# Layer 1 of a four-layer graph network as a nested polynomial in adj, two pairs of batches at a time, and the comparisons and mask values of the softmax on GpSimd

## The chip, the cores and the metric

The kernel runs on one core of one Trainium2 chip. The metric is the device time of a whole execution in microseconds (us). Runs are compared with runs of the kernel before, taken on the same chip in the same rounds.

## The reference, cut to what matters

`x` has 32 batches of 512 nodes and 128 features; `adj` is a sparse, non-negative 512x512 matrix. Each of four layers is a layer norm, a ReLU, a graph operation and a residual.

```python
# layer 0: a softmax over the columns where adj > 0; entry number k in row order gets e[k]
m = adj > 0
idx = jnp.cumsum(m.reshape(-1).astype(jnp.int32)) - 1
vals = e[0][idx].reshape(adj.shape)          # e has 256 entries, later ones repeat the last
A = jax.nn.softmax(jnp.where(m, vals, NEG), axis=1)
out = einsum('ij,bjg->big', A * M, h0) + einsum('ij,bjg->big', A * (1.0 - M), h1) + bias
# layer 1: Chebyshev hops of order 2, for A1 = A2 = adj
x1 = einsum('bnf,nw->bwf', x0, A)
x2 = 2.0 * einsum('bnf,nw->bwf', x1, A) - x0
out = relu(concat(X, x1, x2, x1, x2) @ Theta1 + bias)
# layer 2: messages through adj * adj (elementwise), two projections;  layer 3: masked attention
```

## The kernel before: the parts that matter

Two batches form a pair `q`, 16 pairs in all. A product with a 512x512 matrix is a seven-product scheme over 2x2 blocks. Three banks (a, c, d) take the seven products, and a bank is written again as soon as its reader has taken the last sum out:

```python
ORDER = ((1, "a", True), (6, "c", True), (5, "d", True), (7, "c", False), (2, "a", False),
         (4, "c", False), (3, "d", False))

def products(name, form, left, right, evict):
    banks = {}
    for k, g, first in ORDER:
        if first:
            banks[g] = bank(f"p_{name}_{g}")
        form(banks[g], left[k], right[k], first)      # TensorE
        evict(k, banks[g])                            # VectorE, or ScalarE for 1 and 2
        yield
```

Layer 1 forms `cheb` = 2 adj^2 - 1 once and then, for each pair, multiplies by adj and by cheb, **interleaved two by two**:

```python
def layer1(q):
    h = normed(q)
    yield
    hT = transposed(h, f"hT1_{q}")                    # VectorE and DMA
    right = right_blocks(..., f"h_{q}", [nc.gpsimd] * 4)  # four differences on GpSimd, rt_h
    yield
    mixes = (mixed(f"x1T_{q}", sums["adj"], right, x1T, ...),
             mixed(f"x2T_{q}", sums["cheb"], right, x2T, ...))
    for _ in zip(*mixes):
        pass
    hs = [straight(hT, b, None, f"hs_{q}_{b}") for b in range(2)]
    yield
    for b in range(2):                                # three projections, summed in a bank
        po = projected(..., (columns(hs[b]), th[:, 0, :]), (columns(x1T[:, b]), th12[:, 0, :]),
                       (columns(x2T[:, b]), th12[:, 1, :]))
        ...                                           # bias, relu, residual on VectorE
    ln_stats(q)
```

The softmax preparation, cut to the four comparisons and the values of unmasked entries:

```python
for t in range(NT):
    s = prep.tile([P, NE], F16, tag="lt", name=f"lt_{t}", bufs=2)
    nc.vector.tensor_scalar(s, cols[:, :NE], incl[:, t : t + 1], None, OP.is_lt)
    nc.vector.scalar_tensor_tensor(of_row[:, t, :], cols[:, :NE], before[:, t : t + 1], s,
                                   OP.is_ge, OP.mult)
...
nc.tensor.matmul(ph, identh, m[:, t, :], start=False, stop=True)   # the mask, for each t
```

The order of work between the layers is that of a list of generators; each step of the list advances all active ones in turn, and an engine takes its instructions in the order in which they were issued (some reordering by a scheduler apart):

```python
waiting = [[next_layer, layer0_last(), layer1(1)]]
waiting += [[layer1(q)] for q in range(2, NQ)]
waiting[5].append(square())
waiting[-1].insert(0, layer2(0))                      # layer 2 begins ahead of layer 1's last pair
waiting += [[layer2(q)] for q in range(1, NQ)]
```

## Time and profile before

| Landmark in the trace (us from the span's start) | before |
|---|---|
| row counts of adj known (`incl`) | 7.43 |
| first product of layer 0 | 35.74 |
| second product of layer 0 | 40.05 |
| first product of layer 1 | 196.49 |
| first score product of layer 3 | 686.91 |
| end of the span | 972.16 |
| **median time of three runs** | **974.61** |

The landmarks are the starts of records in TensorE's timeline (`incl` is from VectorE's). They cut the span into parts, so that a change of the total can be put down to a part. The profile's other lines stand in the prediction. Columns are start, us, engine, line, operation, tiles, shapes, records and, in brackets, the idle time before and its releaser.

### The profile page before, as it was taken

To read this page: it belongs to the slowest core of one execution; us is meant where nothing else is said; L and a number is where in the kernel's file an instruction comes from. 1 tells how busy PE (TensorE), PEld (TensorE's weight loads), DVE (VectorE), ACT (ScalarE), POOL (GpSimd) and SP (SyncE) were. 2 spreads that over 40 slices of the span, in tenths; PEclk is the share of its full clock that TensorE was granted. 3 is DMA by queue.
4 is the path that set the end of the run, shared out by engine and by line. 5 is a ranking of instruction groups with operands and counts; after the bars stand their busy time and mean duration, and the time that the engine had idled before them with its cause. 6 is when DMAs were issued, how large, how long until landed. Compare 5 with 4: busy or idle time off the path is not lost.

```text
span 972.2 us, 15193 instructions
## 1 busy us (share of the span) xinstructions
PE 963.8 (99%) x5477; PEld 786.5 (81%) x5478; DVE 591.7 (61%) x1367; ACT 467.6 (48%) x1056; POOL 396.4 (41%) x447
## 2 busy tenths in 40 slices
PE   8999999999999999999999999999999999999998
PEld 4789999899999999999977777777676777777776
DVE  8768887755555655557756666656554444444444
ACT  5765456022323223248676644455674455444553
POOL 5658798932244222221244443334142333223322
DMA  9155554511241221235343433332132121121111
GB/s 261 49 152 152 153 151 116 145 37 51 97 121 44 71 61 50 81 87 140 80 123 114 126 94 87 86 87 75 54 91 64 45 76 55 55 77 44 55 33 44
DMA packets 83050, 87.10 MB, mean 90 GB/s; under 512 B 6816, under 2 KB 73120, under 8 KB 82976
## 3 DMA queue, kind: packets, MB, share of 16 engines
q1 hardware_dynamic: 82976, 86.14, 31.3%
q8 instruction: 43, 0.70, 0.3%
q14 instruction: 31, 0.25, 0.1%
HBM read 44.70 MB, written 41.42 MB: 89 GB/s over the span
## 4 chain that ended last, share of the span: by engine, by line
PE 95%; DVE 2%; ACT 1%; POOL 0%; DMA 0%; issue 0%; DVEq 0%; ACTq 0%
PE p_av L956 12%; PE p_l L406 12%; PE p_score L941 11%; PE p_msgT_c L351 5%; PE p_x1T_c L351 4%; PE p_x2T_c L351 4%; PE p_l_c L358 4%; PE p_feat L406 3%; PE p_msgT_d L351 3%; PE p_x1T_a L351 3%; PE p_msgT_a L351 3%; PE p_hv L406 3%; PE p_x2T_d L351 3%; PE p_x1T_d L351 3%; PE p_x2T_a L351 3%; PE p_g L406 3%
## 5 line engine op out<-in xcount | busy, mean ns | idle before, releaser
L233 ACT ACTIVATE h<-x,sh,rs 128x128 f32<-128x128 f32 x512 | 208.8, 483 | 90.0 <-PE p_x2T_d L351 46.6
L946 POOL TENSOR_TENSOR ex<-ex,adjTx 128x512 f32<-128x512 f32 x64 | 83.2, 1301 | 206.4 <-ACT ex L944 200.8
L942 ACT ACTIVATE ex<-p_score 128x512 f32<-128x512 f32 x128 | 71.9, 587 | 124.6 <-issue 113.0
L956 PEld LDWEIGHTS p_av<-qkh_hv,ex 128*128 128x128 f32 x1024 | 118.5, 191 | 9.4 <-issue 7.4
L956 PE MATMUL p_av<-qkh_hv,ex 128*128 128x129 f32 x1024 | 120.1, 275 | 0.8 <-POOL ex L946 0.8
L941 PE MATMUL p_score<-qkh_hv,hT 128*128 128x512 f32 x256 | 115.2, 593 | 0.0
L267 DVE STREAM_TRANSPOSE hb_hT<-h 128x512 f32<-128x512 f32 x122 | 83.1, 696 | 20.0 <-ACT h L233 18.5
L946 DVE TENSOR_TENSOR ex<-ex,adjTx 128x512 f32<-128x512 f32 x64 | 45.4, 709 | 81.8 <-ACT ex L944 81.8
L205 DVE BATCH_NORM_STATS2 bn<-x 128x6 f32<-128x256 f32 x256 | 93.0, 418 | 1.6
L941 PEld LDWEIGHTS p_score<-qkh_hv,hT 128*128 128x128 f32 x256 | 46.2, 190 | 46.5 <-issue 45.0
L406 PE MATMUL p_l<-th,x12T 128*128 128x128 f32 x512 | 78.1, 275 | 0.0
L944 ACT ACTIVATE ex<-ex 128x512 f32<-128x512 f32 x128 | 76.6, 630 | 1.9
L332 POOL TENSOR_TENSOR rt_h<-h 128x256 f32<-128x256 f32 x32 | 23.3, 727 | 114.2 <-PE p_x2T_d L351 66.8
L406 PEld LDWEIGHTS p_l<-th,x12T 128*128 128x128 f32 x512 | 67.5, 192 | 0.0
L332 POOL TENSOR_TENSOR rt_feat<-feat,feat 128x256 f32<-128x256 f32 x16 | 11.6, 727 | 126.1 <-ACT feat L894 126.1
L666 POOL COPY hs<-hT 128x512 f32<-128x512 f32 x32 | 19.6, 614 | 74.5 <-PE p_l L406 32.9
L406 PE MATMUL p_l<-th,hs 128*128 128x128 f32 x256 | 49.5, 275 | 0.0
L406 PEld LDWEIGHTS p_hv<-vw,hT 128*128 128x128 f32 x256 | 33.6, 192 | 15.3 <-issue 8.1
L906 POOL TENSOR_TENSOR x<-x,phi2b 128x256 f32<-128x256 f32 x64 | 45.0, 735 | 0.0
L379 ACT COPY x12T<-p_x1T_a 128x256 f32<-128x256 f32 x16 | 6.0, 372 | 74.5 <-PE p_x1T_a L351 74.5
L406 PEld LDWEIGHTS p_l<-th,hs 128*128 128x128 f32 x256 | 40.0, 192 | 0.8
L961 DVE SCALAR_TENSOR_TENSOR x<-p_av,rsum,x 128x128 f32<-128x128 f32 x128 | 39.1, 347 | 1.9
(225 smaller groups left out, 1978.6 us busy)
## 6 DMA issues: line engine op xcount, KB each, us to landing
d_hT<-hb_hT SPq DMA_DIRECT2D x244, 128.0 KB
hT<-d_hT SPq DMA_DIRECT2D x61, 512.0 KB
x<-in_x_dram SPq DMA_DIRECT2D x32, 256.0 KB
out_dram<-x SPq DMA_DIRECT2D x31, 256.0 KB
adj_s<-in_adj_dram SPq DMA_DIRECT2D x4, 256.0 KB
adjT_d<-adjT SPq DMA_DIRECT2D x1, 1024.0 KB
sq<-in_adj_dram SPq DMA_DIRECT2D x4, 256.0 KB
adjTx<-adjT_d SPq DMA_DIRECT2D x4, 256.0 KB
```

What stands on the lines that cost most here:

```text
L205: nc.vector.bn_stats(st[:, k].rearrange("p e s -> p (e s)"), xt[q][:, b, t : t + 2, :].rearrange("p t f -> p f t"))
L233: nc.scalar.activation(h[:, b, t, :], xt[q][:, b, t, :], AF.Relu, bias=shift[q][:, i : i + 1], scale=scale[q][:, i : i + 1])
L267: nc.vector.transpose(hb[:, :, b].rearrange("p j t r -> p t j r"), h[:, b].rearrange("p t (j c) -> p t j c", c=QR))
L351: nc.tensor.matmul(p[:, :H], b[:, k, :], a[:, k, :], start=(first and k == 0), stop=(k == 1), skip_group_check=True)
L406: nc.tensor.matmul(p[:, blk(t)], hT(t), w, start=(i == 0), stop=(i == len(terms) - 1))
L906: tc.keep_in_program_order(nc.gpsimd.tensor_add(xi, xi, spread(phi2b, 2)))
L941: nc.tensor.matmul(ps, hT[:, t, b, :], qkh, start=True, stop=True)
L942: nc.scalar.activation(ex[:, t, :], ps, AF.Tanh, scale=1.0 / (8.0 * math.sqrt(D)))
L944: nc.scalar.activation(ex[:, t, :], ex[:, t, :], AF.Exp, scale=8.0)
L946: eng.tensor_mul(ex[:, t, :], ex[:, t, :], adjTx[0][:, t, :])
L956: nc.tensor.matmul(po[:, i, : D + 1], ex[:, t, blk(i0 + i)], hv[:, t, :], start=(t == 0), stop=(t == NT - 1))
L961: nc.vector.scalar_tensor_tensor(xi, po[:, i, :D], rsum[:, i0 + i : i0 + i + 1], xi, OP.mult, OP.add)
```

## The change

Layer 1 is written as x Theta' + adj (x Theta'' + adj x Theta'''), so that adj squared is never formed. For two pairs at a time, one multiplication by adj gives x1T, a two-term projection gives `w`, ScalarE copies it out, GpSimd forms its four differences, and a second multiplication by adj gives tokens, to which the own term is added. Every multiplication by adj now stands alone. In the softmax, the comparisons go to GpSimd, and so does adding the unmasked entries' value to the mask (`entries`), which saves a TensorE product for each row block. The transposes of adj move behind the counts. Cut to its core:

```diff
-    s = prep.tile([P, NE], F16, tag="lt", name=f"lt_{t}", bufs=2)
-    nc.vector.tensor_scalar(s, cols[:, :NE], incl[:, t : t + 1], None, OP.is_lt)
+    s = prep.tile([P, NE], F16, tag="lt", name=f"lt_{t}", bufs=4)
+    nc.gpsimd.tensor_scalar(s, cols[:, :NE], incl[:, t : t + 1], None, OP.is_lt)
 ...
+    def entries(t):
+        nc.scalar.mul(us[t], m[:, t, :], elastn)
+        nc.gpsimd.tensor_add(att[:, t, :], us[t], att[:, t, :])
 ...
-        nc.tensor.matmul(ph, identh, m[:, t, :], start=False, stop=True)
 ...                                        # cheb_rows and its calls go
-    def layer1(q):
-        ...
+    def layer1(r):                          # pairs A = 2r and C = 2r + 1
+        h[A] = normed(A)
+        yield
+        turned(A)                           # transpose by DMA, rt_h on GpSimd
+        h[C] = normed(C)
+        yield
+        first(A)                            # mixed(x1T), alone
+        turned(C)
+        yield
+        first(C)
+        weighed(A)                          # two-term projection, nc.scalar.copy to w1
+        yield
+        weighed(C)
+        right2 = right_blocks(... w1 ..., f"w_{r}", [nc.gpsimd] * 4)     # rt_w
+        yield
+        for _ in products(f"l1_{r}", by_token, sums["adj"], right2, evict):
+            pass
+        ...                                 # own term, bias, relu, residual, statistics
-    waiting = [[next_layer, layer0_last(), layer1(1)]]
-    waiting += [[layer1(q)] for q in range(2, NQ)]
+    waiting = [[next_layer, layer0_last()], [layer1(1)]]
+    for r in range(2, NQ // 2):
+        waiting += [[], [layer1(r)]]
     waiting[5].append(square())
-    waiting[-1].insert(0, layer2(0))
+    waiting[-1].append(layer2(0))
```

## The prediction

> **What bounds the kernel now.** I read the page's busy shares first, then the groups of matmuls by shape, then the chain of work that ended last, then the timelines of TensorE, VectorE, ScalarE and GpSimd over the first 62 us.
>
> ```profile
> PE 963.8 (99%) x5477; PEld 786.5 (81%) x5478; DVE 591.7 (61%) x1367; ACT 467.6 (48%) x1056; POOL 396.4 (41%) x447
> ```
>
> TensorE looks busy all the time, and nobody else is near it. Because the ends of matmuls are modelled, I check this with starts, in the chain of waits:
>
> ```profile
> 36.16 0.62 ACT adiag L650
> 36.77 2.68 ACT h L233 x7
> ...
> 40.21 1.74 PE p_l_c L358 x8
> ...
> 208.75 5.36 PE p_l L406 x48
> 226.19 5.36 PE p_l L406 x48
> 243.64 5.36 PE p_l L406 x48
> ```
>
> From about 40 us the chain is nearly all TensorE, and layer 1 repeats every 17.45 us. Before 40 us the chain runs through VectorE and ScalarE. So there are two regimes: a preparation of some 40 us bound by a chain of small steps, then 929 us bound by the number of matmul columns.
>
> The columns' price comes from the starts in TensorE's timeline. 48 records of 128 columns take 5.36 us, 0.1117 each; 8 records of 256 take 1.73 us, 0.216 each; 4 of 512 take 1.72 us, 0.430 each. A float32 product is two records (24 calls in the code are 48 records), a transpose is one. So a product costs 0.223, 0.432 or 0.860 us at 128, 256 or 512 columns. Check: layer 1 has 28 products of 256 and 24 of 128 for each pair of batches, 12.10 + 5.36 = 17.46 us, and the period is 17.45. Layer 1 has no gap at all today.
>
> **What the Trainium skill says.**
> 1. "TensorE: Matmul & The Clock Gate", Back-to-back issue gap: spacing is about N/2.4 ns + 2.5 warm, N/1.2 cold. At 512 columns this is 216 ns; the bf16 products of the softmax preparation run at 1.30/6 = 0.217 us here, so the trace agrees for bf16. For float32 the trace shows 0.430 for each of two records, and I use that.
> 2. Same page, Part 1: TensorE starts at half rate, returns to it after an idle window of some 3.4 us, and needs about as long at work to speed up. The first transposes here go at 3.65/16 = 0.228 us, the later ones (p_attT, 12 in 1.34 us) at 0.11: agrees. It matters below.
> 3. "GPSIMD Engine Reference", Engine selection: one-input elementwise work runs at about line rate there, two-input work about half as fast as VectorE. Here a two-input 128x512 operation takes 1.28 us on GpSimd against 0.69 on VectorE, and the one-input mask row 0.62: agrees.
> 4. "PSUM — Partial Sum Buffer", PSUM bank collisions: two engines must not touch one bank at once, so a product that reuses a bank waits for its reader. The trace shows such waits in layer 2 (below).
>
> **The change part by part.**
>
> *Forming twice adj squared minus one.* It is 16 products of 512 columns:
>
> ```profile
> L456 PE MATMUL p_cheb<-adj_s,adjT 128*128 128x512 f32 x32 | 14.8, 595 | 0.0
> ...
> L591 PE MATMUL p_first<-m,identh 128*128 128x512 bf16 x3 | 1.1, 379 | 0.0
> ```
>
> 16 x 0.860 = 13.8 us of TensorE vanish, but not 13.8 us of time. Where they stand decides:
>
> ```profile
> 8.63 1.88 PE L456 MATMUL p_cheb<-adj_s,adjT 128*128 128x512 f32 x4
> 10.35 1.89 PE L511 MATMUL p_row<-m,of_row 128*128 128x512 bf16 x8
> 12.08 0.34 PE L514 MATMUL p_before<-befh,of_row 128*128 128x1 bf16 x8
> 12.28 5.40 PE L456 MATMUL p_cheb<-adj_s,adjT 128*128 128x512 f32 x12
> ...
> 41.78 1.88 PE L456 MATMUL p_cheb<-adj_s,adjT 128*128 128x512 f32 x4
> ...
> 62.71 1.88 PE L456 MATMUL p_cheb<-adj_s,adjT 128*128 128x512 f32 x4
> ```
>
> The first 16 records (6.9 us) fill time in which TensorE would wait for VectorE: worth nothing. The other 16 (four groups at 41.8, 48.7, 59.2 and 62.7 us) stand in the saturated part: 4 x 1.72 = **-6.9 us**.
>
> *Layer 1 nested.* The old sum of three terms becomes: one 7-product multiply by adj to features (14 x 0.432 = 6.05 us for each pair), a two-term projection (16 x 0.223 = 3.57), a second 7-product multiply by adj that gives tokens (28 products for two pairs, 6.05 each pair), and the own term (8 x 0.223 = 1.79). Sum 17.46 us. **The columns are exactly those of before, so layer 1's work does not shrink: 0 us.** What changes is its form: half the multiplications now stand alone instead of interleaved two by two (rival B).
>
> *Start of layer 0.* Pair 3 is turned on TensorE rather than by VectorE and DMA: 8 transposes x 0.11 = +0.9 us. Making adiag (8 records, +0.9) moves from the filler before the first product into the saturated part. In exchange the transposes of pair 2, which waited for its normalisation on ScalarE, come later. Before, the first product starts at 35.74 and lasts 1.73, the transposes need 0.87, yet the second starts only at 40.1: 1.8 us of waiting. After, the second product waits for sums that VectorE has at 37.3 and GpSimd's difference at 37.2, just as the first ends: **-1.8 us**. Sum of this part: 0.9 + 0.9 - 1.8 = 0.
>
> *Softmax preparation.* VectorE is its chain:
>
> ```profile
> 7.91 0.28 DVE L507 TENSOR_SCALAR lt<-cols,incl 128x256 f16<-128x256 f16 x1
> 8.22 0.48 DVE L508 SCALAR_TENSOR_TENSOR of_row<-cols,before,lt 128x256 bf16<-128x256 f16 x1
> 8.62 0.28 DVE L507 TENSOR_SCALAR lt<-cols,incl 128x256 f16<-128x256 f16 x1
> ```
>
> Moving the four comparisons shortens each 0.72 us step to about 0.45 us (estimate from the starts): some 1.1 us, and 0.2 us since the counts no longer queue behind the transposes of adj. The mask product leaves TensorE: 0.216 of the 1.94 us that one row block takes (24.54 to 26.49), 0.8 us over four. That would be -2 us. Against it: (i) GpSimd gets four additions of 1.28 us and ScalarE four scalings of about 0.6. Two scalings stand between the halves of pair 1's normalisation, ahead of the first exponential. Laying ScalarE's order out with the durations above, I get the first exponential at about 24.9 us instead of 24.15, and the last scaling at about 31 instead of 31.4. (ii) Without the filler TensorE has little work from 13 to 18 us and may run the score products at half rate: eight at 0.43 instead of 0.217 is +1.7 us per row block, for one or two blocks. Net: **0 us, with -2 to +2 possible.**
>
> **Sum without new waits:** -6.9 + 0 + 0 + 0 = -6.9, that is 967.7 us.
>
> **The rivals.**
>
> *A. The whole 13.8 us come off, and the preparation gains 2 us besides.* For: TensorE is 99% busy. Against: that share counts the filler, and the preparation is paced by VectorE. It would give about 958 to 960 us.
>
> *B. New bank waits in layer 1.* A lone multiplication returns to its bank after one other product, 0.86 us. The reader needs 0.43 us plus some 0.25 until it starts. Layer 2 already works that way:
>
> ```profile
> 649.80 1.13 PE L351 MATMUL p_msgT_c<-sq,rt_feat 128*128 128x256 f32 x4
> ...
> PEld p_msgT_c L351 <- DVE u_msg L373: 3.5, 10, 0.4
> ```
>
> In its first half no time is lost (13.05 us from p_feat at 534.46 to the next), in its second half 0.24 us (13.29 from 640.07 to 653.36), when VectorE or ScalarE comes late. With two such places in each of 16 multiplications and VectorE 58% busy in layer 1 (156 of 270 us), I expect about 0.12 us each: 16 x 0.12 = **+2 us**, 0 to 5. Alone it makes about 970.
>
> *C. Bubbles at the links of the nest.* The second multiplication needs both pairs weighed, copied out (0.6 us each on ScalarE) and their four differences on GpSimd (4 x 1.28). The second product's difference is ready about 3.9 us after the weighing; between stand a multiplication of the next two pairs (6.05) and the first product (1.73), 7.8 us. GpSimd is at 26% in layer 1. So this should be hidden; if the order of work fails, 2 to 4 us in each of 8 rounds: 985 to 1000 us.
>
> *D. Cold TensorE and a longer ScalarE chain in the preparation:* up to +3 us, which with B makes 973 to 975.
>
> **Range and chances.** -6.9 from the columns, +2 from B gives -4.9: 969.7, and I say **969.5 us**. Low end: no bank waits and a preparation 2 us shorter, a little more for an undisturbed join of layers, 963.5. High end: B at 5 us, D at 3, and something of C, 977. Faster by over 2% needs under 955, more than even rival A gives: 0.02. Slower by over 2% needs over 994, only with C: 0.03. Within 2%: 0.95.
>
> **What would show it.** Right: no p_cheb records; layer 1's products in the same total number and pace (34.9 us for two pairs, plus a few tenths); the first layer 0 product near 35 to 36 us and the second right after it; waits of x1T's bank on VectorE of some tenths, 16 or 32 times; score products at 0.43 us at their start if TensorE is cold. Wrong: a layer 1 round well over 36 us, with TensorE waiting for GpSimd differences or for the copied weighed tile (C); a preparation shorter by over 3 us (then A was nearer); or gaps in the first layer 0 round, since GpSimd is 82% busy from 40 to 190 us.

## More of the kernel before

One more view matters afterwards: TensorE's timeline where layer 0 ends and layer 1 begins, and where layer 1 ends and layer 2 begins.

```profile
197.36 1.03 PE L351 MATMUL p_x2T_a<-cheb,h 128*128 128x256 f32 x4
198.22 1.03 PE L351 MATMUL p_x1T_c<-sums_adj,rt_h 128*128 128x256 f32 x4
...
201.68 1.03 PE L351 MATMUL p_x1T_c<-adj_s,rt_h 128*128 128x256 f32 x4
...
478.29 1.03 PE L351 MATMUL p_msgT_c<-sums_sq,rt_feat 128*128 128x256 f32 x4
```

None has a bracket: both joins run without a wait. The layer 1 products alternate between x1T and x2T.

## The result, and the profile after

The changed kernel takes **990.40 us** (median of 6 runs, 988.74 to 991.60), the kernel before 974.59 (6 runs, 974.41 to 975.45). The ratio is 1.0160, with a 95% interval of 1.0147 to 1.0173. A ratio is the mean time of one kernel's runs over that of the other's runs of the same rounds, so it is not quite the ratio of the medians. All outputs are right. The change costs 1.6%. That is within 2%, the most likely class, but it is a loss of 15.8 us where I had predicted a gain of 5, 20.9 us from my 969.5 and outside the range. The execution that was profiled is the slowest of the six (991.60), so the parts below add up to more than 15.8.

The page's busy line of the changed kernel, against the one in the prediction:

```profile
PE 960.1 (97%) x5449; PEld 783.5 (79%) x5450; DVE 582.9 (59%) x1312; ACT 473.9 (48%) x1058; POOL 439.6 (44%) x482
```

TensorE is busy 3.7 us less than before and yet the span is 17.4 us longer: the work did shrink, and waits came in. The landmarks say where:

| Landmark | before | after | difference |
|---|---|---|---|
| `incl` | 7.43 | 8.76 | +1.33 |
| first product of layer 0 | 35.74 | 39.12 | +3.38 |
| second product of layer 0 | 40.05 | 41.05 | +1.00 |
| first product of layer 1 | 196.49 | 192.96 | -3.53 |
| first score product of layer 3 | 686.91 | 704.06 | +17.15 |
| end of the span | 972.16 | 989.55 | +17.39 |

Layer 0 gains 4.53 us from its second product on. Layers 1 and 2 lose 20.68. Layer 3 is as it was (+0.24). TensorE's timeline of the changed kernel shows the waits one by one:

```profile
19.80 3.17 PE L249 MATMUL p_hT<-ident,h 128*128 128x128 f32 x8 [3.64 <-ACT h L231]
...
192.96 1.03 PE L349 MATMUL p_x1T_a<-adj_s,h 128*128 128x256 f32 x4
...
198.29 2.05 PE L349 MATMUL p_x1T_c<-adj_s,rt_h 128*128 128x256 f32 x4 [2.57 <-DVE rs L217]
...
242.69 1.10 PE L349 MATMUL p_x1T_c<-adj_s,rt_h 128*128 128x256 f32 x4 [0.32 <-DVE rs L217]
...
476.15 2.08 PE L349 MATMUL p_msgT_c<-sums_sq,rt_feat 128*128 128x256 f32 x4 [5.41 <-POOL rt_feat L330]
```

I price each by the distance between starts, less what the same records take when warm (0.864 us for four of 256 columns):

- **Join of layers 0 and 1:** 2.74 us of waiting before 198.29, then eight records at half rate, 0.98 and 0.69 us: **4.4 us**.
- **Rounds of layer 1:** from one round of two pairs to the next (starts of p_l_e from 237.63 to 451.87) six rounds take 214.24 us, 35.63 each and once 36.09, against 6 x 34.90 before: **4.8 us**.
- **Join of layers 1 and 2:** 0.85 us before 469.61, 5.68 us before 476.15, then twelve records at half rate, 2.7 us: **9.2 us**.
- One gap in the second round of layer 2, at 519.79, where TensorE waits for an eviction: **1.1 us**.

The sum is 19.5 of the 20.7 us; the rest is in pieces of 0.1 to 0.2 us.

The waits at the joins are the same in every experiment below that leaves them alone, but what follows them is not. This is TensorE's timeline in the experiment `e2_lt_vector`, which changes only the preparation:

```profile
195.95 1.10 PE L349 MATMUL p_x1T_c<-adj_s,rt_h 128*128 128x256 f32 x4 [2.57 <-DVE rs L217]
196.89 1.03 PE L349 MATMUL p_x1T_a<-adj_s,h 128*128 128x256 f32 x4
```

After the same wait TensorE goes on at full rate: its granted clock (the share of full speed that the profile reports) is 1.00 from 195.9 to 199.0, against 0.53 from 198.3 to 201.7 in the changed kernel. From layer 1's first product to the first p_l_e it is 43.08 us there and 43.05 in `e4_nest_alone`, against 44.67 here and 44.69 and 44.73 in two more kernels with the same wait. The round with the second join (from 451.87 to 499.69 here, 47.82 us) takes 46.63 to 48.10 us in the kernels that leave it alone. So some 1.5 us at each join come and go without a change to it, and an experiment's gain can't be read closer than that from one profile.

Why the joins wait can be read from the queues ahead of them. First layers 0 and 1. This is GpSimd's timeline and then VectorE's, of the changed kernel:

```profile
194.14 0.73 POOL L330 TENSOR_TENSOR rt_h<-h,rt_h 128x256 f32<-128x256 f32 x1
194.83 1.26 POOL L751 TENSOR_TENSOR x<-x,u_l 128x512 f32<-128x512 f32 x1
```

```profile
196.13 0.69 DVE L833 TENSOR_TENSOR x<-p_l_e,x 128x512 f32<-128x512 f32 x1 [2.62 <-POOL x L751]
196.74 1.09 DVE L203 BATCH_NORM_STATS2 bn<-x 128x6 f32<-128x256 f32 x3
197.74 0.41 DVE L372 TENSOR_TENSOR x1T<-p_x1T_c,x1T 128x256 f32<-128x256 f32 x1
```

Layer 0's last residual addition stands on GpSimd behind the `rt_h` differences of layer 1's first pairs. VectorE's next instruction needs it, and waits 2.62 us. Behind that, in the same queue, stands the eviction that would free bank c, though its sum has been ready since about 194.9. TensorE waits for the bank. The Trainium skill, page "PSUM — Partial Sum Buffer", section "Engine vs sequencer instructions", says that the queues of these engines are strict first-in first-out; the trace agrees, since an eviction whose sum is ready and that needs nothing from GpSimd starts only 1.6 us after GpSimd's addition has ended.

The kernel before has the same late addition, in its GpSimd timeline, and loses nothing, because it needs bank c back later:

```profile
194.40 1.27 POOL L750 TENSOR_TENSOR x<-x,u_l 128x512 f32<-128x512 f32 x1
```

In the changed kernel TensorE is at layer 1 by 3.5 us earlier, while GpSimd is not. And before, two multiplications are interleaved, so that three other products stand between the two uses of bank c (2.6 us) and one more ahead of the first; a lone multiplication leaves one (0.86 us). The second use falls at 201.7 before and would fall at 195.6 after. The bank is free at 198.2 (197.74 and 0.41).

Next layers 1 and 2, GpSimd's timeline of the changed kernel and then a line of ScalarE's:

```profile
468.99 1.27 POOL L330 TENSOR_TENSOR rt_w<-w 128x512 f32<-128x512 f32 x1 [18.57 <-ACT w L872]
...
474.01 0.72 POOL L330 TENSOR_TENSOR rt_feat<-feat,feat 128x256 f32<-128x256 f32 x1
```

```profile
465.41 0.62 ACT L964 ACTIVATE feat<-feat 128x512 f32<-128x512 f32 x1
```

GpSimd does nothing for 18.6 us, because the next thing in its queue is `rt_w`, and that needs the last copy of `w`. Behind it stands `rt_feat`, whose input ScalarE had finished at 466.0. The order comes from one word of the diff: `append` where `insert(0, ...)` was.

Last the preparation, in the chain that ended last. Its columns are start, us, what.

```profile
8.76 0.17 DVE incl L475
...
9.02 3.65 POOL lt L486 x4
...
15.34 1.22 POOL att L519
...
16.65 0.21 POOL sd L210
...
39.12 1.99 PE p_l_a L356 x8
```

The chain now runs through GpSimd: four comparisons of 0.9 us, then the small operations on the entries, then the first `entries` addition, and only then the normalisation of pair 0 (`sd`). Before, this was the GpSimd line, with nothing in the way:

```profile
13.69 0.20 POOL L212 TENSOR_SCALAR sd<-bn 128x8 f32<-128x8 f32 x1 [2.27 <-DVE bn L205]
```

From `incl` to `sd` it is 6.26 us before and 7.89 after.

### The profile page after: what moved, and what is told of

It reads as the page before. It is cut to its first block, busy times and chain, and to the rows that moved or that the text cites. A ratio compares the mean times of both kernels' runs of the same rounds, so it can differ in the third digit from the quotient of the medians.

```text
span 989.5 us, 15113 instructions
## 1 busy us (share of the span) xinstructions
PE 960.1 (97%) x5449; PEld 783.5 (79%) x5450; DVE 582.9 (59%) x1312; ACT 473.9 (48%) x1058; POOL 439.6 (44%) x482
## 4 chain that ended last, share of the span: by engine, by line
PE 84%; POOL 6%; DVE 6%; ACT 2%; issue 1%; DMA 1%; SPq 0%; DVEq 0%; POOLq 0%; ACTq 0%
PE p_av L1025 12%; PE p_score L1010 11%; PE p_l_c L356 7%; PE p_w L405 5%; PE p_msgT_c L349 5%; PE p_l_a L356 5%; PE p_l_d L356 5%; PE p_x1T_c L349 4%; PE p_hv L405 3%; PE p_msgT_d L349 3%; PE p_feat L405 3%; PE p_qkh L997 3%; PE p_l L405 3%; PE p_msgT_a L349 3%; PE p_phi L980 3%; PE p_phi L981 3%
## 5 line engine op out<-in xcount | busy, mean ns | idle before, releaser
L330 POOL TENSOR_TENSOR rt_w<-w 128x512 f32<-128x512 f32 x16 | 20.3, 1269 | 108.2 <-ACT w L872 108.2
L370 ACT COPY x1T<-p_x1T_a 128x256 f32<-128x256 f32 x16 | 5.9, 370 | 94.0 <-PE p_x1T_a L349 94.0
L405 PE MATMUL p_w<-th,x1T 128*128 128x128 f32 x256 | 49.5, 275 | 0.0
L405 PE MATMUL p_w<-th,hs 128*128 128x128 f32 x256 | 49.5, 275 | 0.0
L982 ACT ACTIVATE msgT<-p_phi,phi1b 128x512 f32<-128x512 f32 x32 | 21.7, 678 | 41.0 <-PE p_phi L981 41.0
L405 PEld LDWEIGHTS p_w<-th,hs 128*128 128x128 f32 x256 | 40.1, 192 | 0.8
L964 ACT ACTIVATE feat<-feat 128x512 f32<-128x512 f32 x32 | 20.1, 629 | 42.2 <-DVE feat L963 42.2
L651 POOL TENSOR_TENSOR hd<-hT,adiag 128x512 f32<-128x512 f32 x32 | 39.8, 1272 | 1.2 <-ACT adiag L764 1.2
```

The source lines that it names most:

```text
L405: nc.tensor.matmul(p[:, blk(t)], hT(t), w, start=(i == 0), stop=(i == len(terms) - 1))
```

## The experiments

**Theory:** the columns saved are a gain, as predicted, and the loss is three separate queue orders (the two joins and the rounds) plus GpSimd in the preparation. **Rival 1:** the nest itself is the loss, since its second multiplication must wait for `w`. **Rival 2:** the loss is cold TensorE, or one thing that moves when it is mended. Twelve kernels ran, each told with its edit against the changed kernel unless another is named.

### Which half costs what

First the nest alone: the softmax half is undone (comparisons, mask product and the place of adj's transposes as before).

```diff
-        nc.gpsimd.tensor_scalar(s, cols[:, :NE], incl[:, t : t + 1], None, OP.is_lt)
+        nc.vector.tensor_scalar(s, cols[:, :NE], incl[:, t : t + 1], None, OP.is_lt)
-    entries(0)                              # and entries(1) to entries(3)
+        nc.tensor.matmul(ph, identh, m[:, t, :], start=False, stop=True)
 ...                                        # elastn, the scratch tiles and adj's transposes as before
```

> The changed kernel with the softmax half undone (comparisons on VectorE, mask by a product with the identity, no additions on GpSimd, adj turned early); the nested layer 1 stays. Theory (in the preparation the comparisons on GpSimd cost 1.0 us and the missing filler products, which leave TensorE cold, about 1.5; the mask product saved 0.65): within 1 us of the changed kernel, 989.5 to 990.5 us, because the cold TensorE stays. Rival (the softmax half alone makes the preparation longer): 987 us or less.

Measured: 987.58 us (4 runs, before 974.80), ratio 1.0139 (1.0122 to 1.0156).

Then the softmax half alone, in the kernel before: the same lines the other way round.

```diff
-        nc.vector.tensor_scalar(s, cols[:, :NE], incl[:, t : t + 1], None, OP.is_lt)
+        nc.gpsimd.tensor_scalar(s, cols[:, :NE], incl[:, t : t + 1], None, OP.is_lt)
-        nc.tensor.matmul(ph, identh, m[:, t, :], start=False, stop=True)
+    entries(0)                              # and entries(1) to entries(3)
 ...                                        # elastn and the scratch tiles as in the changed kernel
```

> The kernel before with the softmax half alone (comparisons and mask additions on GpSimd, no identity product); adj squared and the old layer 1 stay, so TensorE has its filler. Theory: +1.0 us from the comparisons, -0.6 from the mask product, nothing from a cold TensorE: 974 to 976 us. Rival (the softmax half lengthens the preparation by over 3 us, by GpSimd and ScalarE): 977.5 us or more. If the halves add, the differences of this and of the nest alone to the kernel before sum to 15.8 us.

Measured: 976.22 us (4 runs), ratio 1.0017 (1.0002 to 1.0032). The two halves add, 1.39% + 0.17% against 1.60%. I had predicted the softmax half to be worth nothing, and it costs 1.7 us alone (0.2 to 3.1 by the interval) and 2.8 within the changed kernel, by medians of runs whose ranges overlap. The nest alone reaches layer 1 at 190.39, 6.1 us earlier than the kernel before (196.49): the predicted -6.9 us of columns are nearly all there, and are lost afterwards.

### The join of layers 1 and 2

```diff
-    waiting[-1].append(layer2(0))
+    waiting[-1].insert(0, layer2(0))
```

> One list operation undone: layer 2's first pair goes before layer 1's last pair in each step, as in the kernel before, so that its four differences (rt_feat) come before the last weighed differences (rt_w) in GpSimd's queue. Theory (queue order at the join of layers 1 and 2): the 5.6 us wait of the first layer 2 multiplication for rt_feat and the half-rate products after it go; about 8.5 us less than the changed kernel, 982 us. Rival (the nest simply drains: the last pair has no other work to cover its copies and differences): the wait moves to the last layer 1 product, under 3 us gained, 987 us or more.

Measured: **979.31 us** (4 runs, before 974.80), ratio 1.0054 (1.0039 to 1.0069). From layer 1's start to layer 3's first score it is 502.31 us instead of 511.10: 8.8 us come back, as the theory says; 0.5 us more lies ahead of layer 1. The median fell by 11.1, more than the two profiles show, since the profiled execution of this kernel was the slowest of its four (982.07). GpSimd's timeline of this kernel has the two in the other order:

```profile
458.27 0.73 POOL L330 TENSOR_TENSOR rt_feat<-feat,feat 128x256 f32<-128x256 f32 x1 [4.37 <-ACT feat L964]
...
474.92 1.28 POOL L330 TENSOR_TENSOR rt_w<-w 128x512 f32<-128x512 f32 x1 [10.99 <-ACT w L872]
```

GpSimd still waits for `w`, now with a layer 2 multiplication on TensorE meanwhile. One line of the schedule is over half of the whole loss.

### The join of layers 0 and 1

First I took GpSimd's queue away as a cause: the differences of the first three pairs go to VectorE.

```diff
-            right[q] = right_blocks(..., [nc.gpsimd] * 4)
+            right[q] = right_blocks(..., [nc.vector if q < 3 else nc.gpsimd] * 4)
```

> The twelve differences of the first three pairs of layer 1 move from GpSimd to VectorE; nothing else. Theory (at the join of layers 0 and 1 the last x additions stand behind twelve rt_h differences on GpSimd, VectorE waits for x, and the eviction of layer 1's first products stands behind that): the 2.7 us wait and the half-rate products after it go, 3.5 to 4.5 us less, 986.4 us. Rival (the end of layer 0 is short of VectorE time, not of GpSimd time): no gain or a loss, 990 us or more.

Measured: 994.28 us (4 runs), ratio 1.0200 (1.0185 to 1.0215). A miss, and an instructive one. TensorE's, VectorE's and GpSimd's timelines of this kernel:

```profile
187.10 3.33 PE L356 MATMUL p_l_c<-rt_g,attT 128*128 128x256 f32 x7 [6.25 <-DVE rs L217]
```

```profile
183.22 0.80 DVE L330 TENSOR_TENSOR rt_h<-h 128x256 f32<-128x256 f32 x1 [5.34 <-POOL hd L651]
```

```profile
178.27 4.92 POOL L651 TENSOR_TENSOR hd<-hT,adiag 128x512 f32<-128x512 f32 x4
```

A difference stands at the head of VectorE's queue for 5.34 us, and now layer 0's evictions stand behind it. It does not wait for `h`, which ScalarE had finished at 163.8. It starts as GpSimd's last `hd` ends (183.19). `hd` reads `adiag`, and in the code `adiag` and the differences take their buffers from one ring of six (`rt`), so that the difference probably waits for that buffer; no run tests this. The join itself ran without a wait here, but layer 0's last round lost more than that. The time lies where the rival said (990 us or more), though for another reason than a VectorE short of time: the wait moved to an engine that has more to lose. So I kept the engine and changed the order: layer 0's last round is issued first, and its additions and the first `rt_h` keep that order on GpSimd.

```diff
-            engs[i].tensor_sub(t[i], p, q)
+            step = engs[i].tensor_sub(t[i], p, q)
+            if name in ("h_0", "h_1", "h_2"):
+                tc.keep_in_program_order(step)
 ...                                        # the same for the last round's additions
-    waiting = [[next_layer, layer0_last()], [layer1(1)]]
+    waiting = [[layer0_last(), next_layer], [layer1(1)]]
```

> The same instructions on the same engines as the changed kernel; in GpSimd's queue the last round's three x additions go before the first three pairs' twelve differences. Having fallen with the move to VectorE (that put the same work into another full queue), the theory is now narrower: it is the place in the queue, not the amount of work. Theory: VectorE's wait for the last x addition (2.6 us) goes, TensorE's 2.7 us wait at the first layer 1 product and its half-rate products after it go: 3.5 to 4.5 us less, about 986.5 us. Rival (GpSimd is simply short of time at the end of layer 0): the differences come late instead and TensorE waits for them; within 1 us of the changed kernel.

Measured: **986.31 us** (4 runs, before 975.07), ratio 1.0115 (1.0101 to 1.0129). The same four records, in TensorE's timeline of this kernel, with no idle time before them:

```profile
194.49 1.10 PE L351 MATMUL p_x1T_c<-adj_s,rt_h 128*128 128x256 f32 x4
```

### The rounds of layer 1

Another order of the seven products puts one more product between two uses of a bank where it helps, and forms the fifth's sum at once.

```diff
+    LONE = ((1, "a", True), (6, "c", True), (5, "d", True), (2, "a", False), (7, "c", False),
+            (3, "d", False), (4, "c", False))
             elif k == 7:
-                nc.vector.tensor_add(m1[2], p, m1[0])
+                nc.vector.tensor_add(m1[2], p, m1[2])
             elif k == 5:
-                return
+                nc.vector.tensor_add(m1[2], p, m1[0])
 ...                                        # the later addition of the fifth's sum goes
```

> The seven products of a lone multiplication to features in another order (1, 6, 5, 2, 7, 3, 4), the fifth evicted at once, so that a bank is reused after two other products instead of one at all but one place; same instructions otherwise. Theory (the 0.5 to 0.95 us waits in each layer 1 round and the 0.2 to 1.1 us ones in layer 2 are bank waits behind VectorE): of 5.5 us lost in layer 1 and 3.5 in layer 2 over half goes: 4 to 6 us less, about 985 us. Rival (VectorE is late for its own reasons): the waits move to another product, under 1.5 us.

Measured: 985.91 us (4 runs, before 975.07), ratio 1.0111 (1.0097 to 1.0125). The time is as expected (985), but only in part for the reason expected, which was waits in the rounds and in layer 2. A round takes 35.45 us instead of 35.63 (six of them 213.51 instead of 214.24), and the 1.1 us gap in layer 2 is gone. The largest part is at the join of layers 0 and 1: two products now stand between the two uses of bank c, and TensorE waits 1.86 us there instead of 2.74, with little half rate after it (2.3 us less in all). The main wait of the round is still there, in TensorE's timeline of this kernel:

```profile
239.64 1.10 PE L352 MATMUL p_x1T_c<-adj_s,rt_h 128*128 128x256 f32 x4 [0.32 <-DVE rs L217]
```

So it was not the bank's distance alone. VectorE had the layer norm's statistics of the round before (`bn`, 1.08 us for three) ahead of the eviction. The last run of the chain below moves them.

### GpSimd in the preparation

The comparisons alone go back to VectorE, with everything else changed:

```diff
-        nc.gpsimd.tensor_scalar(s, cols[:, :NE], incl[:, t : t + 1], None, OP.is_lt)
+        nc.vector.tensor_scalar(s, cols[:, :NE], incl[:, t : t + 1], None, OP.is_lt)
```

> The changed kernel with the four comparisons alone back on VectorE; the mask additions stay on GpSimd. Theory (a comparison takes 0.90 us there and paces the four steps, 0.90 instead of 0.72 each, and starts later): the first product of layer 0 comes 1.0 to 1.3 us earlier, 989.2 us. Rival (the 2.8 us of the softmax half are in the mask additions, which queue before the normalisation factors on GpSimd): under 0.5 us gained.

Measured: 986.73 us (4 runs, before 974.74), ratio 1.0127 (1.0112 to 1.0143), 3.7 us less than the changed kernel and more than expected (989.2). It is also 0.9 less than with the whole softmax half undone, within the spread of the runs. In its profile, 2.34 us of the gain are ahead of layer 1 and 3.06 in layers 1 and 2, which the edit does not touch: mostly the shorter half rate after the joins that was shown above. The chain of this kernel:

```profile
8.48 0.17 DVE incl L475
...
14.68 0.21 POOL sd L210
```

From `incl` to `sd` it is 6.20 us. In all 14 profiles this distance is 6.20 to 6.26 us where the comparisons are on VectorE and 7.86 to 7.89 us where they are on GpSimd. This is the cleanest measure of their cost, 1.6 us on the chain, since `incl` itself lies between 7.41 and 8.76 us. The first `entries` addition is still ahead of `sd` on GpSimd in this kernel, and adds nothing to the distance. That spread comes from when adj's third block lands, in some kernels the fourth too. The kernel before and the last experiment have 7.43 and 7.41, the twelve kernels with a part of the change in them 7.68 to 8.76. Why the block lands later, no run here tells.

Six products without use after the transposes, to keep TensorE warm:

```diff
+    p_warm = bank("p_warm")
+    for i in range(6):
+        nc.tensor.matmul(p_warm, adj_s[:, 0, blk(i % NT)], adj_s[:, 1, :], start=True, stop=True)
```

> The changed kernel with six float32 products of 512 columns, whose result nobody reads, on TensorE behind the transposes of adj (5.2 us of work, where adj squared used to stand); nothing else. Theory (TensorE has gone cold before the score products: 2.77 us for the first six instead of 1.99, first exponent delayed): the first scores run at 0.217 us each and the first product of layer 0 starts 1.0 to 1.5 us earlier; 989 us. Rival (the preparation is paced by VectorE and ScalarE anyway): no change, within 0.3 us.

Measured: 988.80 us (4 runs, before 975.07), ratio 1.0146 (1.0130 to 1.0161): 1.6 us back of 15.8 by the medians, with overlapping ranges. The first six value products take 1.43 us by their starts (22.93 to 24.36) instead of 2.56, and from `sd` to layer 1's first product it is 175.41 us instead of 176.31. Cold TensorE (rival 2, and rival D of the prediction) is real and small, about 0.9 us by the trace.

### All mended together

The softmax half undone, eight fillers (two ahead of the comparisons, six behind the counts), layer 2 first, the join's order kept and the lone order of products, in one kernel. The edits are those above, and for the fillers:

```diff
+    def fill(n):
+        for i in range(n):
+            nc.tensor.matmul(p_warm, adj_s[:, 0, blk(i % NT)], adj_s[:, 1, :], start=True, stop=True)
+    fill(2)                                 # ahead of the comparisons
+    fill(6)                                 # behind p_before
```

> All mendings on the nested layer 1: softmax half undone, eight filler products where adj squared stood in the preparation, layer 2's first pair first, x additions first at the end of layer 0, and the lone order. If the causes are separate and add: 990.4 - 2.8 - 1.5 - 9 to 11 - 4 - 5 = 966 to 968 us, 0.7 to 0.9% under the kernel before, which is the 6.9 us that I predicted from the columns. Rival (each mending uncovers another wait): 972 us or more.

Measured: 973.91 us (5 runs, before 975.07), ratio 0.9991 (0.9978 to 1.0003). Short of the expected 966 to 968, and in the rival's range (each mending uncovers another wait: 972 us or more). Most of what is missing is in layers 1 and 2, from layer 1's first product to layer 3's first score 495.44 us against 490.42 before; six rounds still take 213.49 against 209.40. Some more was left in the preparation, as VectorE's and GpSimd's timelines of this kernel show:

```profile
20.78 3.13 DVE L567 TENSOR_SCALAR at_part<-cols,col_of,part 128x512 bf16<-128x512 f16 x6
```

```profile
22.43 1.33 POOL L414 TENSOR_TENSOR x<-x,b 128x512 f32<-128x512 f32 x1 [2.92 <-ACT h L233]
```

Six one-input operations on 16-bit data take 3.13 us beside a GpSimd addition of 1.33. The Trainium skill, page "SBUF — State Buffer", section "Who interferes with whom", says that a VectorE `tensor_scalar` in a two-port mode and a GpSimd instruction share a port pair, and that whoever issues first holds it for the whole instruction. I tested that by moving the addition.

```diff
     go(normal[1])
-    bias(0)
 ...
     scaled_rows(NT - 1, us[-1])
+    bias(0)
```

> The combined kernel with one addition on GpSimd (the bias of the first x block, 1.33 us) moved from the time of VectorE's at_part comparisons to behind the softmax rows. Theory (VectorE and GpSimd got in each other's way: the six comparisons took 3.13 us there, 2.15 in the kernel before, where the addition ran just after them): at_part back to 2.1 us and the first product of layer 0 1.0 us earlier, 972.9 us. Rival (they were late for something else): at_part stays at 3.1 us, time the same.

Measured: 972.83 us (4 runs, before 974.74), ratio 0.9979 (0.9966 to 0.9993). VectorE's timeline of this kernel:

```profile
21.31 2.02 DVE L566 TENSOR_SCALAR at_part<-cols,col_of,part 128x512 bf16<-128x512 f16 x6
```

1.11 us less with nothing changed but what runs beside it. From `sd` to the first product of layer 0 it is 21.52 us instead of 22.63, the same 1.11, and the median fell by 1.08. The runs show that the overlap costs this time; that the shared ports are the reason is the skill's account of it.

Two more edits on that kernel: the two fillers that ran cold ahead of `p_row` go, and the statistics of a round come one step later.

```diff
-    fill(2)
 ...
         done(p, u[2], 1, 1)
+        yield
         if C == NQ - 1:
             yield
-            yield
         ln_stats(A)
         ln_stats(C)
```

> The combined kernel with the late bias, without the two filler products that ran ahead of the row products, and with the statistics of a finished layer 1 pair one step later, so that they stand behind the evictions of the next lone multiplication in VectorE's queue. Theory (the 0.49 to 0.95 us that stayed in each layer 1 round under the new order are VectorE's statistics in front of the eviction): of 4.9 us left in layer 1 at least 3 go, and 1.3 us in the preparation: 969 to 970 us, 0.5% under the kernel before. Rival (the x updates in front of them are enough to be late): 971.5 us or more.

Measured: **971.80 us** (5 runs, before 974.74), ratio **0.9968 (0.9956 to 0.9981)**. This beats both kernels: by 0.3% the one before, and by about 1.9% the changed one (by the medians). It is short of the expected 969 to 970, and the rival (the x updates in front of the eviction are enough to make it late: 971.5 us or more) has the number. A round is 35.22 us, 0.23 less than in the kernel before it, so the statistics were that part of the wait. Taking the two fillers out gained nothing: from `sd` to layer 0's first product it is 21.51 us, where it was 21.52. Against the kernel before, the first product of layer 0 is at 36.24 (+0.50), that of layer 1 at 190.12 (-6.37), the first score at 684.50 (-2.41). Layers 1 and 2 still give back 4.0 us: 2.4 in six rounds (0.32 each and once 0.79) and the rest in small waits of this kind, in TensorE's timeline:

```profile
272.17 1.10 PE L356 MATMUL p_x1T_c<-adj_s,rt_h 128*128 128x256 f32 x4 [0.30 <-DVE x1T L381]
```

### Could the old kernel have had that gain?

The new order of products was put into the kernel before. There the third scratch tile is not part of the output, and product 7 has to write the output directly. Against the kernel before:

```diff
+    LONE = (...)                            # as above, used in layers 1 and 2
             elif k == 7:
-                nc.vector.tensor_add(m1[2], p, m1[0])
+                nc.vector.tensor_add(dst[:, 1, H:], p, m1[2])
             elif k == 5:
-                return
+                nc.vector.tensor_add(m1[2], p, m1[0])
```

> The kernel before with nothing changed but the order of the seven products of a multiplication (1, 6, 5, 2, 7, 3, 4, the fifth's sum formed at once), as in the best version. It asks whether the 0.32% by which the best version beats the kernel before could be had without the nest. The lone multiplications are only in layer 2 here, and the kernel before loses some 1.9 us there (0.2 and 0.24 us at a time from 560 to 700 us in the trace). If the order mends these, 972.8 us, ratio 0.998; if these waits have another cause (in the lone-order run on the changed kernel, the small ones at 540 to 700 us stayed), no change: 974.6, ratio 1.000. I lean to the second. Then the best version's gain belongs to the nest, mended.

Measured: 974.76 us (5 runs), the kernel before 974.65 (9 runs), ratio 1.0004 (0.9991 to 1.0018). No change. The order of products is worth nothing to the old kernel, so it is not where the best version's 0.3% comes from. Most of the other mends have nothing to act on there: it has neither wait at its joins, and its comparisons are on VectorE. The late bias addition was not tried on it; its six `at_part` operations take 2.15 us, so at most 0.1 us is to be had.

## Why the prediction was wrong, point by point

- **The columns: right.** The product counts, the pace and the saving held. From layer 0's second product to layer 1's first, the changed kernel gains 4.53 us. My terms for that stretch are -6.9 and the adiag (0.9) and eight more transposes for each of two pairs (0.9 each), -4.2.
- **Start of layer 0: right.** I gave -1.8 us of waiting after the first product. The second follows the first by 1.93 us, where it was 4.31.
- **The filler is worth nothing: right,** and the nest alone shows it: without those products, the first product of layer 0 starts at 36.55, no earlier than before.
- **The softmax preparation, "0 us, with -2 to +2 possible": wrong in size, about +2.8 by the medians.** The failing step is "Moving the four comparisons shortens each 0.72 us step to about 0.45 us". It took the rest of the step from VectorE and priced no comparison on GpSimd. One takes 0.90 us there, so a step became 0.90. Besides, I laid out ScalarE's order but not GpSimd's, where the comparisons and the first addition now stand ahead of pair 0's normalisation. The runs showed 1.6 us on the chain for the comparisons (7.86 to 7.89 against 6.20 to 6.26 from `incl` to `sd`).
- **Rival B, the bank waits: right mechanism, mis-sized.** Term: 16 x 0.12 = +2. Measured 4.8 in six of the eight rounds, at the upper end of my 0 to 5. Part of it is not the bank's distance but statistics ahead of the eviction in VectorE's queue (35.45 to 35.22).
- **Rival C, the links of the nest: the step that failed.** I wrote "So this should be hidden", from 7.8 us of other products between the weighing and the second product, and I gave C only "something" of the high end. Within the rounds that holds: no round waits for `rt_w`. It fails after the last pair, where the other work that hides the link is missing: there is no multiplication of the next two pairs (6.05 of my 7.8 us), and what could stand in, layer 2's first multiplication, was queued behind the link on GpSimd. That is 9.2 us.
- **The first join: not in the prediction.** Its 4.4 us are no link of the nest. TensorE waits for bank c, the place that rival B names, but B was priced in the steady state at 0.12 us, and here the reader came 2.74 us late, because layer 0's last additions were behind layer 1's differences on GpSimd. My sum has no term for either join; the one join that I mention is a possible gain at the low end. I had checked durations and distances in the steady state, and not the queue orders at the joins, though the diff changes the schedule's lines there. The two joins cost 4.4 + 9.2 = 13.6 us. The two experiments on them gave back 4.1 and 11.1 us in their medians.
- **Rival A** (all 13.8 us come off): refuted, as expected.
- **Rival D** (cold TensorE): 0.9 us (trace) to 1.6 us (medians) at the start by the fillers, and 0.98 + 0.69 + 2.7 = 4.4 us that follow the waits of the joins and are counted there.

With the joins at +13.6, B at +4.8 instead of +2 and the preparation at +2.8 instead of 0, my 969.7 becomes 988.9, and 990.0 with the 1.1 us gap in layer 2, against 990.4 measured. These are sizes read after the event, those of the joins from the slowest execution, and the half rate after the joins varies by some 1.6 us; that the sum meets the measurement within 1 us is partly luck. But each of the four was tested by a run of its own. Rival 1 of the experiments, that the nest must lose, is refuted: mended, it is faster than the kernel before. What stays open is why adj's blocks land 0.3 to 1.3 us later in the changed programs, where the remaining 0.3 us of a round go in detail, and what decides how long the half rate lasts after a wait.

## What to carry to other kernels

A link in a pipeline that is hidden in the steady state has to be checked again at the first and the last round, because the work that hides it belongs to a neighbour that is not there; read the queue of each engine in order across the join, and ask what stands at its head and for what it waits. Two interleaved products hide more than overlapped time: they give every bank's reader three products of slack instead of one, and small lateness elsewhere stays unseen until the interleaving goes. Moving work to an idle engine has a price in three places: its duration there, what it then stands ahead of in that queue, and what it slows on the engine that shares its ports.

## What the Trainium skill lacked or had wrong

- "GPSIMD Engine Reference", section "Engine selection": one-input work there is called roughly line rate. A comparison of 256 fp16 columns against a per-partition value took 0.90 us on GpSimd against 0.28 on VectorE, 3.5 ns for a column. The mask row, with constants, took 0.62 us for 512, 1.2 ns for a column. Which of the operand, the type or the comparison makes the difference, no run here tells.
- "SBUF — State Buffer", section "Who interferes with whom": it holds here, and gives ratios but no time for a pair like this. Six `at_part` operations took 2.02 us alone and 3.13 us beside one GpSimd addition of 1.33 us.
- "TensorE: Matmul & The Clock Gate", Part 1: an idle window of about 3.4 us is given for the return to half rate. Here a shorter one, 2.57 us in the profile (2.74 by the starts), was followed by eight records at half rate (3.4 us for what takes 1.73 warm; granted clock 0.53), and 5.41 us by twelve. In `e2_lt_vector` the same 2.57 us were followed by full rate (granted clock 1.00). Why, no run here tells.
- No page draws the consequence that an eviction can be held up in its engine's queue by an unrelated instruction that waits for a third engine. The first-in first-out rule is on "PSUM — Partial Sum Buffer", and what came of it here was 2.6 us on VectorE and 18.6 us on GpSimd.
